# Joining the transfers of a convolution and Haar kernel: slanted filter rows, image blocks, channel parities, v with tau

## The chip, the cores and the metric

The kernel runs on one core of a Trainium2 chip. The metric is the device time of one execution in microseconds. Before the change the median of three runs is 2617.15 us (2612.36 to 2619.04). About 0.3% of that, some 8 us, is what a measurement of this kernel can tell from no change.

## What is computed

A tensor x of 4 images, 64 channels and 256 x 256 points (float32) goes through four layers. Layers 0, 2 and 3 are long convolutions whose filter is an outer product of a row filter and a column filter for each channel, so that each is a product with a Toeplitz matrix along the columns and then one along the rows, and `+ x * bias[c]`. The filters themselves come from a small network of three sines:

```python
h = sin(freq * (z @ w1 + b1)); h = sin(freq * (h @ w2 + b2)); h = sin(freq * (h @ w3 + b3))
hx = (h @ wo) * decay          # the same for hy with Y weights
k[c, i, j] = hx[i, c] * hy[j, c]
y = irfft2(rfft2(x) * rfft2(k)) [:256, :256] + x * bias[c]
```

Layer 1 works in the two-dimensional Haar domain, with two sets of weights i:

```python
f1 = haar2d(x)
for i in range(2):
    f4 = einsum("bchw,oc->bohw", f1 * v[i], conv_w[i])
    acc += sign(f4) * relu(abs(f4) - tau[i])
x = haar2d(acc, inverse=True) + x
```

## The kernel before, in words

The work is cut into rounds. A round holds two images (a group) and CI = 2 channels, as a tile of 128 partitions by 8 x 256; there are 64 rounds, 32 for each of the two groups. Three kinds of work follow each other and partly run side by side, in an order that Python loops write out (`beside` interleaves two lists of pieces, with no scheduler behind it):

- Phase A, for each round: layer 0 as two Toeplitz products on TensorE (`rows` into the PSUM tile a1ps, `columns` into a2ps, 128 matmuls each), the residual on VectorE (L449), the Haar butterflies along the free axis on GpSimd (L333, L335), the Haar product a3ps on TensorE, its scaling on VectorE (L462), and a store of the coefficients to DRAM (L466).
- Phase B, for each group and each of 64 steps: a step loads one slab of coefficients (L528, ft), v and tau (L539), mixes channels on TensorE (L579), multiplies by v (VectorE, L594), takes sign and magnitude (ScalarE, L598, L602), subtracts tau and thresholds (VectorE, L605, L608), adds up on GpSimd (L620 to L624), and stores to the DRAM tensor `mixed` (L629). Before its first mix, `join` finishes the Haar transform of steps 0 and 1 on VectorE (L551 to L558).
- Phase C, for each round: loads from `mixed` (L692, g), inverse Haar (GpSimd L370, ScalarE L353, TensorE c0ps), and layers 2 and 3 as Toeplitz products (c1r, c1c, c2r, c2c), with copies on ScalarE (L733) and residuals on VectorE (L752), and a store to `out` (L759).

In time: A runs alone up to some 450 us, A beside B of group 0 up to 1030 us, a transition to C up to 1200 us, C beside B of group 1 up to 1930 us, and C alone to the end.

The Toeplitz matrices are made by DMA. `spread` (L248) writes each channel's filter, zero padded to PERIOD = 320, REPEATS = 20 times into the DRAM tensor `filt`, and `load_toeplitz` (L139) reads it back with a slanted pattern (partition p starts p elements earlier), 64 partitions at a time, into tx (both X filters of a round) and ty (the Y filters). For rounds 0 and 1 `repeated` (L212) computes the copies directly, ahead of the network's last layer.

All DMAs are issued by the queue of SyncE (SP), in the order of the program; each takes one of eight semaphores in turn and so waits for the DMA eight places before it. What an issue also waits for is a buffer (tx and ty have 5, ft 4, v and tau 3, the x and g tiles 3) or data (a filter row that has landed in `filt`, coefficients). The lists `rest` and `thirds` (L270 to L274) place the `spread` calls of later quarters, and the networks of layers 2 and 3, between the pieces of phase A.

## Time and profile before

The profiled execution took 2622.7 us; its span, first to last instruction, is 2620.6 us, so 2.1 us lie around it.

| | busy us | share of the span |
|---|---|---|
| TensorE matmul (PE) | 2357.1 | 90% |
| TensorE weight load (PEld, overlaps PE) | 1908.0 | 73% |
| GpSimd (POOL) | 1951.1 | 74% |
| VectorE (DVE) | 1686.6 | 64% |
| ScalarE (ACT) | 1325.3 | 51% |

The granted TensorE clock is 0.965 on average. The DMA engines moved 631.58 MB in 241180 packets, 241 GB/s on average; the hardware queue's packets fill 69.4% of the 16 engines' span. Of a DMA the profile tells the issue (an instruction of SPq, the queue of SyncE), its count and its KB. A share of busy time is an average over stages whose limits differ, so it is read stage by stage.

### The profile page before, as it was taken

Reading aid. Unit: us, or ns where it says so; the run is one execution under the profiler, and the core shown is the slowest. Engines: PE = TensorE matmul, PEld = TensorE weight load, DVE = VectorE, ACT = ScalarE, POOL = GpSimd, SP = SyncE. Lnnn points to the kernel's source line nnn. Section 1 sums busy time; section 2 is a strip of 40 time slices with the busy share of each in tenths; the row PEclk is TensorE's granted clock in tenths of the full one; section 3 lists DMA queues with packets and bytes.
Section 4 is the critical chain, followed back from the end, with each engine's and each line's share of the span. In section 5 each row is a group of like instructions: output and inputs, shape, how many; then the busy total and the mean of one; then the engine's idle time right before and its main releaser. Section 6 shows DMA issues by size and latency. Waiting matters only on the chain.

```text
span 2620.6 us, 120068 instructions
## 1 busy us (share of the span) xinstructions
PE 2357.1 (90%) x53276; PEld 1908.0 (73%) x53276; DVE 1686.6 (64%) x1972; ACT 1325.3 (51%) x2169; POOL 1951.1 (74%) x2422
## 2 busy tenths in 40 slices
PE   6989999678878778768999999999999999999999
PEld 4777777445544445546877777787789999999999
DVE  2464445799999999736877878878763333333333
ACT  1111112566666656426777776778763443434432
POOL 2877887888989989858888878888876565565661
PEclk9999999899899888979999999999999999999999
DMA  5756887698999889556888878888865544445442
GB/s 147 252 193 221 254 261 275 232 332 326 336 332 335 319 316 331 186 190 216 286 310 288 295 273 288 274 285 286 284 231 181 171 143 153 159 141 166 148 137 86
DMA packets 241180, 631.58 MB, mean 241 GB/s; under 512 B 42758, under 2 KB 125351, under 8 KB 224536
## 3 DMA queue, kind: packets, MB, share of 16 engines
q1 hardware_dynamic: 240664, 623.92, 69.4%
q8 instruction: 419, 6.86, 1.1%
q14 instruction: 97, 0.79, 0.1%
HBM read 412.59 MB, written 211.16 MB: 238 GB/s over the span
## 4 chain that ended last, share of the span: by engine, by line
PE 42%; DVE 12%; DMA 10%; POOL 9%; ACT 6%; issue 5%; SPq 2%; DVEq 0%; ACTq 0%; POOLq 0%
PE c1c L285 9%; PE c2r L285 9%; PE c2c L285 8%; PE c1r L285 8%; PE c0ps L297 3%; DVE a L605 3%; PE f L579 3%; DVE x L594 3%; POOL f L335 2%; POOL fw L333 2%; DVE m L608 2%; DMA ft<-coef 2%; ACT a L602 2%; DMA mixed<-gt 2%; DVE x L449 2%
## 5 line engine op out<-in xcount | busy, mean ns | idle before, releaser
L370 POOL TENSOR_TENSOR i<-i,g 128x16 f32<-128x16 f32 x744 | 395.1, 550 | 378.9 <-ACT g L353 359.9
L579 PE MATMUL f<-ft,mix 64*64 64x512 f32 x2048 | 326.4, 642 | 106.7 <-DVE x L594 84.5
L285 PEld LDWEIGHTS a1ps<-tx,x 64*64 64x64 f32 x8192 | 303.4, 140 | 132.9 <-DVE f L462 47.8
L602 ACT ACTIVATE a<-x 128x1024 f32<-128x1024 f32 x256 | 264.5, 1033 | 205.6 <-DVE m L608 205.6
L285 PE MATMUL a1ps<-tx,x 64*64 64x192 f32 (+3 forms) x8192 | 341.5, 309 | 29.3 <-DVE f L462 15.3
L605 DVE TENSOR_TENSOR a<-a,tau 128x1024 f32<-128x1024 f32 x256 | 314.3, 1228 | 79.9 <-ACT a L602 77.5
L285 PEld LDWEIGHTS c2r<-tx,cy 64*64 64x64 f32 x8192 | 319.1, 135 | 62.2 <-ACT ch L733 28.8
L598 ACT ACTIVATE m<-x 128x1024 f32<-128x1024 f32 x256 | 271.9, 1062 | 173.3 <-DVE x L594 112.4
L594 DVE TENSOR_TENSOR x<-f,v 128x1024 f32<-128x1024 f32 x256 | 311.7, 1218 | 61.1 <-PE f L579 56.4
L285 PEld LDWEIGHTS c1c<-ty,ch 64*64 64x64 f32 x8192 | 311.3, 133 | 53.4 <-ACT ch L733 29.8
L285 PE MATMUL c2r<-tx,cy 64*64 64x64 f32 (+3 forms) x8192 | 330.9, 301 | 13.6 <-ACT ch L733 10.9
L285 PE MATMUL c1r<-tx,z 64*64 64x128 f32 (+3 forms) x8192 | 326.7, 299 | 13.1 <-DMA tx<-filt 6.7
L285 PEld LDWEIGHTS c1r<-tx,z 64*64 64x64 f32 x8192 | 303.0, 134 | 46.4 <-issue 26.4
L285 PEld LDWEIGHTS a2ps<-ty,ay 64*64 64x64 f32 x8192 | 281.4, 135 | 74.1 <-issue 27.2
L285 PE MATMUL a2ps<-ty,ay 64*64 64x256 f32 (+3 forms) x8192 | 319.1, 301 | 12.5 <-ACT ay L429 9.1
L285 PE MATMUL c1c<-ty,ch 64*64 64x192 f32 (+3 forms) x8192 | 321.1, 298 | 7.0 <-ACT ch L733 6.2
L608 DVE SCALAR_TENSOR_TENSOR m<-a,m 128x1024 f32<-128x1024 f32 x256 | 313.0, 1223 | 19.5
L429 ACT COPY ay<-a1ps 128x512 f32<-128x512 f32 x256 | 137.0, 587 | 370.7 <-PE a1ps L285 370.3
L285 PE MATMUL c2c<-ty,ch 64*64 64x192 f32 (+3 forms) x8192 | 316.4, 297 | 3.6 <-issue 3.6
L285 PEld LDWEIGHTS c2c<-ty,ch 64*64 64x64 f32 x8192 | 303.2, 133 | 22.4 <-issue 10.9
L449 DVE SCALAR_TENSOR_TENSOR x<-x,bias_sb,a2ps 128x512 f32<-128x512 f32 x256 | 179.4, 743 | 214.1 <-POOL f L335 132.1
L620 POOL TENSOR_TENSOR gt<-gt,m 128x1024 f32<-128x1024 f32 x128 | 303.2, 2369 | 11.7 <-DVE m L608 10.2
(69 smaller groups left out, 3193.9 us busy)
## 6 DMA issues: line engine op xcount, KB each, us to landing
coef<-f SPq DMA_DIRECT2D x256, 256.0 KB, 4.4
ft<-coef SPq DMA_DIRECT2D x256, 256.0 KB, 6.2
v<-in_v SPq DMA_DIRECT2D x128, 512.0 KB, 5.9
tau<-in_tau SPq DMA_DIRECT2D x128, 512.0 KB, 6.6
mixed<-gt SPq DMA_DIRECT2D x256, 256.0 KB, 5.9
g<-mixed SPq DMA_DIRECT2D x256, 256.0 KB, 5.5
x<-in_x SPq DMA_DIRECT2D x63, 1024.0 KB, 8.5
out<-o SPq DMA_DIRECT2D x63, 1024.0 KB, 5.1
```

The source lines that it names most:

```text
L285: nc.tensor.matmul(ps[r][half(c), j % 2, k * ROW :], data[half(r), c, k, bass.ts(j, ROW)], t(r, c)[:, : N - k * ROW], start=k == 0, stop=k ...
L297: nc.tensor.matmul(ps[r][half(c)].rearrange("p h k -> p (h k)"), matrix[half(r)], pairs(r, c).rearrange("p h k -> p (h k)"), start=True, s ...
L370: engine.tensor_tensor(to, s, d, op)
L429: later(lambda y=y, ps=ps: nc.scalar.copy(y, ps))
L449: nc.vector.scalar_tensor_tensor(to, old, bias_sb[:, c : c + 1], ps, ALU.mult, ALU.add)
L579: nc.tensor.matmul(un[u]["f4"][half(q), b, :], mixers[0][half(r), bass.ts(i, C)], st[s]["f"][half(r), b], start=True, stop=True, tile_posi ...
L594: nc.vector.tensor_tensor(un[u]["x"], un[u]["f4"], both(u, "v"), ALU.mult)
L598: nc.scalar.activation(un[u]["m"], un[u]["x"], AF.Sign)
L602: nc.scalar.activation(un[u]["a"], un[u]["x"], AF.Abs)
L605: nc.vector.tensor_tensor(un[u]["a"], un[u]["a"], both(u, "tau"), ALU.subtract)
L608: nc.vector.scalar_tensor_tensor(un[u]["m"], un[u]["a"], 0.0, un[u]["m"], ALU.max, ALU.mult)
L620: nc.gpsimd.tensor_tensor(st[s]["g"], st[s]["g"], m, ALU.add)
```

## The change

Every kind of transfer that was cut in two or more is made one, or fewer:

- `filt` is laid out by round: for each round and each half r of the 128 partitions, 20 repeats of three filters side by side (X of the first channel, X of the second, Y of channel r). One slanted row of 896 elements then holds all three, and a round's Toeplitz data is 2 DMAs of 64 x 896 in place of 6 of 64 x 256, in one tile `toep` with 4 buffers.
- `spread` therefore writes each X filter twice, for r = 0 and r = 1: six DMAs for a quarter of a layer, each with 8 rounds (6 in the first) by 20 repeats by 320. Before it was two DMAs for each of three thirds of the repeats, with 16 channels each. `rest` has 77 entries in place of 44.
- `repeated` computes 120 rows (2 x 20 x 3) in place of 80 and stores them by one DMA in place of two.
- `all_rows` (coefficient stores of A, g loads of C) gives 2 pairs in place of 4: both image halves h in one.
- `step_of` (ft loads, mixed stores of B) gives one transfer in place of two: both channel parities e.
- v and tau are stacked on the host into one tensor and come by one DMA of 1 MB in place of two of 512 KB.

The program has 1245 DMAs in place of 2651. The order of the instructions on the compute engines is the same, apart from where the pieces of the second network stand in phase A.

```diff
@@ -56,7 +56,10 @@
 NL = len(CONV)
 
 PERIOD = N + ROW
+ITEMS = 3
+SPAN = ITEMS * PERIOD
 REPEATS = 20
+COPIES = 2 * REPEATS * ITEMS
 
 FIRST = 2
 
...
@@ -103,7 +106,7 @@
 
     coef = [coefficients(f"coef{g}") for g in range(GROUPS)]
     mixed = [coefficients(f"mixed{g}") for g in range(GROUPS)]
-    filt = [dram.tile([P, REPEATS, PERIOD], F32, tag=f"filt{l}", name=f"filt{l}") for l in range(NL)]
+    filt = [dram.tile([ROUNDS, 2, REPEATS, ITEMS, PERIOD], F32, tag=f"filt{l}", name=f"filt{l}") for l in range(NL)]
 
     def pool(name, bufs, stack=ctx, **kw):
         return stack.enter_context(tc.tile_pool(name=name, bufs=bufs, reuse_waits="tile", **kw))
...
@@ -140,20 +143,12 @@
 
 
 
-        tx = ac.tile([P, CI, N], F32, tag="tx", name=f"tx{l}_{t}", bufs=5)
-        ty = ac.tile([P, N], F32, tag="ty", name=f"ty{l}_{t}", bufs=5)
-
-        def rows(dst, w, e):
-            start = (w * C + t % ROUNDS * CI + e) * REPEATS * PERIOD
-            src = bass.AP(filt[l].tensor, filt[l].offset + start, [[PERIOD - 4, 16], [PERIOD - 1, 4], [1, N]])
-            nc.sync.dma_start(dst, src)
-
-        for e in range(CI):
-            for r in range(2):
-                rows(tx[r * ROW : (r + 1) * ROW, e, :], 0, e)
-        for e in range(CI):
-            rows(ty[e * ROW : (e + 1) * ROW, :], 1, e)
-        return tx, ty
+        both = ac.tile([P, SPAN - ROW], F32, tag="toep", name=f"toep{l}_{t}", bufs=4)
+        for r in range(2):
+            start = filt[l].offset + (t % ROUNDS * 2 + r) * REPEATS * SPAN
+            src = bass.AP(filt[l].tensor, start, [[SPAN - 4, 16], [SPAN - 1, 4], [1, SPAN - ROW]])
+            nc.sync.dma_start(both[r * ROW : (r + 1) * ROW], src)
+        return both
 
 
     early = ctx.enter_context(ExitStack())
...
@@ -211,14 +206,11 @@
 
         def repeated(r):
 
-            ps = mps.tile([4 * REPEATS, N], F32, tag="ps", name=f"mlp_first{r}")
+            ps = mps.tile([COPIES, N], F32, tag="ps", name=f"mlp_first{r}")
             nc.tensor.matmul(ps, wo_first_sb[:, r], st["h"][:, 0], start=True, stop=True)
             t = repeats[r]
             nc.vector.tensor_tensor(t[:, :N], ps, decay_first_sb[:, r], ALU.mult)
-            for w in range(2):
-                to = filt[0][w * C + r * CI : w * C + (r + 1) * CI].rearrange("c r e -> (c r) e")
-                nc.sync.dma_start(to, t[w * CI * REPEATS : (w + 1) * CI * REPEATS])
-
+            nc.sync.dma_start(filt[0][r].rearrange("h c k e -> (h c k) e"), t)
 
         def last():
             ps = mps.tile([P, n, N], F32, tag="ps", name=f"mlp_out{ls[0]}")
...
@@ -240,19 +232,20 @@
 
     filters = {}
     first_toep = []
-    repeats = [mp.tile([4 * REPEATS, PERIOD], F32, tag=f"first{r}", name=f"first{r}") for r in range(FIRST)]
+    repeats = [mp.tile([COPIES, PERIOD], F32, tag=f"first{r}", name=f"first{r}") for r in range(FIRST)]
     for t in repeats:
         nc.gpsimd.memset(t, 0.0)
-    QUARTER = C // 4
-
-    def spread(l, q, part=slice(0, REPEATS)):
-
-        begin = q * QUARTER if (l, q) != (0, 0) else FIRST * CI
-        for w in range(2):
-            s = slice(w * C + begin, w * C + (q + 1) * QUARTER)
-            src = filters[l][s].unsqueeze(1)
-            times = part.stop - part.start
-            nc.sync.dma_start(filt[l][s, part], src.to_broadcast([src.shape[0], times, PERIOD]))
+    QUARTER = ROUNDS // 4
+
+    def spread(l, q):
+
+        begin, end = q * QUARTER if (l, q) != (0, 0) else FIRST, (q + 1) * QUARTER
+
+        def put(r, k, channel):
+            src = filters[l][channel + CI * begin : channel + CI * (end - 1) + 1 : CI].unsqueeze(1)
+            nc.sync.dma_start(filt[l][begin:end, r, :, k], src.to_broadcast([end - begin, REPEATS, PERIOD]))
+
+        return [lambda r=r, k=k: put(r, k, k if k < CI else C + r) for r in range(2) for k in range(ITEMS)]
 
     first_x = [load_x(0)]
     forward_sb = const.tile([P, ROW], F32, tag="forward", name="forward_sb")
...
@@ -267,11 +260,10 @@
     for p in network([0]):
         p()
 
-    thirds = [slice(0, 7), slice(7, 14), slice(14, REPEATS)]
-    rest = [lambda q=q, k=k: spread(0, q, k) for q in range(1, 4) for k in thirds]
+    rest = [p for q in range(1, 4) for p in spread(0, q)]
     rest.append(lambda: wbd_sb.extend(constant(f"wbd{l}", wbd[:, l], [P, 3, P]) for l in (1, 2)))
     rest += network([1, 2])
-    rest += [lambda l=l, q=q, k=k: spread(l, q, k) for l in (1, 2) for q in range(4) for k in thirds]
+    rest += [p for l in (1, 2) for q in range(4) for p in spread(l, q)]
 
     TILES = [(r, c) for r in range(2) for c in range(2)]
 
...
@@ -304,10 +296,10 @@
             )
 
     def filters_x(toep):
-        return lambda r, c: toep[0][half(r), c]
+        return lambda r, c: toep[half(r), c * PERIOD : c * PERIOD + N]
 
     def filters_y(toep):
-        return lambda r, c: toep[1][half(r)]
+        return lambda r, c: toep[half(r), CI * PERIOD :]
 
     def forward_free(src, dst, name):
 
...
@@ -393,13 +385,12 @@
     def all_rows(grp_tile, r, images):
 
 
-        parts = images.rearrange("(m q) (h n) k -> h q m (n k)", q=2, h=2)
+        parts = images.rearrange("(m q) (h n) k -> q m h (n k)", q=2, h=2)
         n = NB * W
         pairs = []
-        for h in range(2):
-            for q in range(2):
-                at = grp_tile.offset + ((h * 2 + q) * ROUNDS + r) * n
-                pairs.append((bass.AP(grp_tile.tensor, at, [[PAIR, P // 2], [1, n]]), parts[h][q]))
+        for q in range(2):
+            at = grp_tile.offset + (q * ROUNDS + r) * n
+            pairs.append((bass.AP(grp_tile.tensor, at, [[PAIR, P // 2], [2 * ROUNDS * n, 2], [1, n]]), parts[q]))
         return pairs
 
     def phase_a():
...
@@ -474,7 +465,8 @@
                     filters(1)
                     load(0)
                     load(1)
-                    spread(0, 0)
+                    for put in spread(0, 0):
+                        put()
                 filters(t + 2)
             if j < BLOCKS:
                 if t < total:
...
@@ -515,28 +507,25 @@
         def step_of(ap, s, images):
 
             n = NB * W
-            by_e = images.rearrange("(m e) b w -> e m (b w)", e=CI)
-            at = [ap.offset + (e * STEPS // 2 + s // 2) * PAIR + s % 2 * P // CI * n for e in range(CI)]
-            return [(bass.AP(ap.tensor, at[e], [[n, P // CI], [1, n]]), by_e[e]) for e in range(CI)]
+            at = ap.offset + s // 2 * PAIR + s % 2 * P // CI * n
+            rows = bass.AP(ap.tensor, at, [[n, P // CI], [STEPS // 2 * PAIR, CI], [1, n]])
+            return rows, images.rearrange("p b w -> p (b w)")
 
         def load_f(s):
             if s >= STEPS:
                 return
             d = st[s]
             d["f"] = bp.tile([P, NB, W], F32, tag="ft", name=f"ft_{grp}_{s}", bufs=4)
-            for rows, f in step_of(coef[grp], s, d["f"]):
-                nc.sync.dma_start(f, rows)
+            rows, f = step_of(coef[grp], s, d["f"])
+            nc.sync.dma_start(f, rows)
 
         def load_v(s):
             if s >= STEPS:
                 return
-            n = 2 * W
-            d = st[s]
-            for name, src in (("v", v), ("tau", tau)):
-                t = d[name] = bp.tile([P, 2, W], F32, tag=name, name=f"{name}_{grp}_{s}", bufs=3)
-
-                rows = bass.AP(src.tensor, src.offset + s * P * n, [[n, P], [1, n]])
-                nc.sync.dma_start(t.rearrange("p e w -> p (e w)"), rows)
+            n = 4 * W
+            t = bp.tile([P, 2, 2, W], F32, tag="v", name=f"v_{grp}_{s}", bufs=3)
+            st[s]["v"], st[s]["tau"] = t[:, 0], t[:, 1]
+            nc.sync.dma_start(t.rearrange("p k e w -> p (k e w)"), bass.AP(v.tensor, v.offset + s * P * n, [[n, P], [1, n]]))
 
         def four(name, at, b):
 
...
@@ -625,8 +614,8 @@
             un[u].clear()
 
         def store(s):
-            for to, g in step_of(mixed[grp], s, st[s]["g"]):
-                nc.sync.dma_start(to, g)
+            to, g = step_of(mixed[grp], s, st[s]["g"])
+            nc.sync.dma_start(to, g)
             st[s].clear()
 
         def piece(u, j):
...
@@ -907,9 +896,10 @@
     scaled = signs * w[order][:ROW, None] / math.sqrt(N)
     signs = signs * w[order][:ROW, None]
     pack = a["L1_conv_conv_w"].transpose(2, 0, 1).reshape(C, P)
-    v = by_row("v")
-
-    filters = [np.repeat([w * C + r * CI + e for w in range(2) for e in range(CI)], REPEATS) for r in range(FIRST)]
+    v = np.stack([by_row("v"), by_row("tau")], axis=2)
+
+    filters = [[r * CI, r * CI + 1, C + r * CI + h] for r in range(FIRST) for h in range(2)]
+    filters = np.tile(np.array(filters).reshape(FIRST, 2, 1, ITEMS), (1, 1, REPEATS, 1)).reshape(FIRST, COPIES)
     wo = _blocks(a[CONV[0] + "Xwo"], a[CONV[0] + "Ywo"])
     arrays = {
 
```

More of the change, by code (lines that the diff above doesn't have):

```diff
@@ L90, in conv_haar_kernel @@
 def conv_haar_kernel(
-    ctx: ExitStack, tc: tile.TileContext, x, zT, w1, wbd, cols, decay, wo_first, decay_first, bias, forward, inverse, wrow, pack, v, tau, out
+    ctx: ExitStack, tc: tile.TileContext, x, zT, w1, wbd, cols, decay, wo_first, decay_first, bias, forward, inverse, wrow, pack, v, out
 ):
@@ L172, in conv_haar_kernel @@
     wbd_sb = [constant("wbd0", wbd[:, 0], [P, 3, P])]
-    wo_first_sb = constant("wo_first", wo_first, [P, FIRST, 4 * REPEATS])
-    decay_first_sb = constant("decay_first", decay_first, [4 * REPEATS, FIRST, N])
+    wo_first_sb = constant("wo_first", wo_first, [P, FIRST, COPIES])
+    decay_first_sb = constant("decay_first", decay_first, [COPIES, FIRST, N])
     decay_sb = constant("decay", decay, [P, N])
@@ L946 @@
         "v": f(np.repeat(v[:, :, None], C, axis=2)),
-        "tau": f(np.repeat(by_row("tau")[:, :, None], C, axis=2)),
     }
```

## The prediction

> **What bounds the kernel now.** I read the busy times by stage first, because the change touches DMAs everywhere and a DMA is worth something only where an engine waits for one. Columns after the stretch: its length, then busy us of PE, PEld, DVE, ACT, POOL, then clock, DMA share, GB/s.

> ```profile
> 0.00:65.00 65.00, 38.91 (x745) 31.65 (x749) 17.71 (x37) 9.21 (x17) 13.03 (x24) 0.95 0.52 144
> 65.00:450.00 385.00, 357.72 (x8845) 285.25 (x8840) 197.30 (x293) 72.31 (x135) 312.02 (x521) 0.99 0.74 239
> 450.00:1030.00 580.00, 457.69 (x7473) 281.46 (x7471) 534.39 (x551) 359.36 (x448) 513.58 (x568) 0.91 0.88 318
> 1030.00:1200.00 170.00, 132.48 (x2338) 92.85 (x2334) 105.30 (x153) 62.66 (x96) 115.95 (x157) 0.87 0.59 209
> 1200.00:1930.00 730.00, 687.31 (x15236) 563.49 (x15228) 577.81 (x585) 549.31 (x883) 611.71 (x625) 0.99 0.81 283
> 1930.00:2621.00 691.00, 683.01 (x18676) 653.25 (x18668) 254.07 (x357) 272.42 (x594) 384.77 (x532) 1.00 0.47 150
> ```

> A alone is bound by PE (93%), A beside B by DVE (92%), C beside B by PE (94%), C alone by PE (99%). Only the start and the transition have an engine that nothing saturates. Next, the list of waits, for every engine wait that a DMA ended; these are its large entries (total, times, longest):

> ```profile
> DVE spare_f L551 <- DMA ft<-coef: 17.4, 1, 17.4
> ACT g L353 <- DMA g<-mixed: 16.0, 2, 12.6
> PE a1ps L285 <- DMA x<-in_x: 9.4, 2, 7.4
> PE c1r L285 <- DMA tx<-filt: 6.7, 1, 6.7
> ```

> With the smaller ones (3.4 for w_sb, 2.9 for tx, and some 25 us on DVE, ACT and POOL) that is all. So although the chain of waits gives DMAs 10% of the span, some 260 us, engines stood waiting for DMAs for about 80 us, and PE, which sets the end of most stages, for 22. The timeline shows two places. The start, with the SP queue:

> ```profile
> 28.37 0.59 SPq L136 DMA_DIRECT2D x<-in_x  x1
> 29.05 2.12 SPq L255 DMA_DIRECT2D filt<-padded  x2
> 36.21 3.51 SPq L149 DMA_DIRECT2D tx<-filt  x4
> 41.04 0.59 SPq L136 DMA_DIRECT2D x<-in_x  x1
> ```

> The x of round 2, issued at 41.04, is what PE waits 7.4 us for, until 50.0. It stood behind the filter rows of round 2, and these behind the landing of `spread` at 36.2. And the transition into C beside B:

> ```profile
> 1156.97 2.50 SPq L149 DMA_DIRECT2D tx<-filt  x4
> 1160.98 7.08 PE L285 MATMUL c1r<-tx,z 64*64 64x256 f32 x120 [6.73 <-DMA tx<-filt]
> 1166.16 4.96 SPq L528 DMA_DIRECT2D ft<-coef  x8
> 1170.55 0.42 DVE L551 TENSOR_TENSOR spare_f<-ft 64x256 f32<-64x256 f32 x1 [17.44 <-DMA ft<-coef]
> 1174.26 0.42 DVE L553 TENSOR_TENSOR spare_f<-ft 64x256 f32<-64x256 f32 x1 [2.83 <-DMA ft<-coef]
> ```

> Here SP issues back to back from 1151.95 on, one DMA in 0.6 us: the reader sees `ft` only reach the queue at 1166.16.

> [...] tx takes 592 ns (median of 768), and the issues of all 2651 DMAs add up to some 1730 us, 77% of the time from 1200 to 1900. [...]

> **The change, part by part.** *Bytes and packets.* In the trace's packet records a packet of 1024 bytes takes 46 ns (median), 4096 takes 159, 8192 takes 309: nearly a straight line, 7 ns and 0.037 ns a byte. v with tau as 8192 in place of twice 4096 saves 9 ns of 318. A slanted row of 3584 bytes comes by the line to 140, against 3 x 46 = 138. So the DMA engines gain nothing by size, and the 88% of A beside B stays. Hidden by DVE there.

> *SP.* 1406 issues fewer. At 0.6 us each that frees 840 us of SP; if a joined issue costs 1.0 us (the first `spread` took 1.06 with 240 rows) still 340. Almost all is nothing on the path: in A alone x is issued when DVE releases its buffer (SP waits 50.8 us on L449 there) and 12 us, a round, before use, with 4.3 to 7.0 us left after landing in the five rounds where the trace tells the landing; in B, v and ft follow DVE's subtraction. Without that cover a late load would cost its lateness each round.

> *Start.* Before: rows of rounds 0 and 1 are 12 issues from 20.71 to 28.3, then x of round 1 at 28.37. After: 4 issues, x at about 24. PE's wait for that x, 2.0 us at 33.6, goes. `spread` then starts 4.3 us earlier (24.7), but holds 720 packets of 1280 bytes in place of 480[...] it lands between 35 and 42, before 36.2. Two issues and one `spread` later x of round 2 is issued at 37 to 44 (before 41.04). With the same 9 us PE starts round 2 at 46 to 53 in place of 50.0. I take the middle with x landing faster, as less is queued beside it: -3 us (+3 to -6).

> *A alone.* `spread` has 66 DMAs of 160 packets, 2.46 in a round of 11.85 us[...]. x is issued first in the round and has 4 us or more to spare: 0, with a bad end below. The 4 buffers of `toep` add no wait in A: they wait for `columns` two rounds back, which precedes the DVE release that the x load ahead already waits for.

> *Transition.* The joined coefficient store must wait for both halves h, so for the last of the four L462 (end 1153.12); the two halves went from 1151.95 to 1154.36. Two issues of 0.6 from 1153.2 end at the same 1154.4. Then g takes 2 issues in place of 4 (1155.6) and the rows 2 in place of 6: the first lands by its 3.9 us at 1159.5 to 1160.5, as the same 2 MB are ahead of it in the engines. PE's 6.73 shrinks by 1. Then rows of layer 3 and the mixer, 3 issues; ft follows at about 1159 (coefficients must have landed) in place of 1166.16, 4 issues. Both steps land by 1167, so `join`, whose last wait ended at 1174.26, ends 7 us sooner. PE waited for it 4.5 us in two pieces (the list has `PE f` on `DVE ft`: 3.5 at 1179.28). These go, and nothing in PE's order before that mix needs it: 1 + 4.5. After it PE waits 4.8 us at 1229 for GpSimd's ci, which starts behind ScalarE's copies of the same mix: half a microsecond of that. Sum -6 (-1 to -11: nothing of join, or all three waits).

> *C beside B.* PE is idle 43 us of 730, mostly on ScalarE's c1r and c2r copies. The DMA waits there (4.6 DVE, 4.5 ACT before it, 8.9 POOL, 1.6 DVE) reach PE in part. I take a fifth of the 15 after 1200: -3 (0 to -8). The 4 buffers make layer 3's rows wait for the end of the last round's columns, not its middle; the next thing in the queue, the `out` store, waits longer than that, and the rows are due over a round later. Freeing v with tau costs nothing: the tau load already came second.

> *C alone.* PE 99%: 0.

> Sum: -3 - 6 - 3 = -12. Against the profiled 2622.7 that is 2610.7. That execution is 5.5 above the median of the runs, so the median becomes 2617.15 - 12 = 2605.

> **Rivals.** (1) *Hidden anyway*: `spread` lands late at the start (+2), and the transition only trades ft for g and ScalarE (-3): 2616. For it: 80 us of waits in 2620, most off PE. Against it: the two PE waits stand plainly at DMAs. (2) *SP's order matters everywhere*: with SP free, half of PE's 43 us in C beside B goes (-20) beside the 9: 2588. For it: SP is 77% busy there and in order, and the chain of waits runs through its issues. Against it: the engines' own lists name compute. (3) *Slower[...]*: [...] +38 - 12: 2643. [...] For it: the mean in A alone is already 112. [...]

> **How the numbers follow.** Main case 0.56, own range 2594 to 2612; hidden 0.23 (2609 to 2620); more 0.08; slower 0.13. The range 2588 to 2620 holds main and hidden and little else, 8 in 10. Faster by over 0.3% (below 2609.3): 0.52 + 0.08 = 0.60. Within: 0.04 + 0.23 = 0.27. Slower (above 2625): 0.13.

> **What would show it.** Round 2's first a1ps before 50.0; the first join of group 1 within 1168 and no PE wait for it; PE idle of C beside B 40 or less; A's round still 11.85 us with no a1ps wait for x; DVE still 92% from 450 to 1030; C alone 691. Wrong if a1ps waits for x or toep in A, or if the joined issues take 1.2 us or more.

## The result and the profile after

The changed kernel takes 2639.47 us (median of 4 runs, 2634.71 to 2646.05) against 2616.24 of the kernel before beside it: ratio 1.0092 [1.0063, 1.012]. Run again later it gave 1.0075 [1.0056, 1.0094]. The kernel before, timed once more beside itself (`before_again`), gave 1.0003 [0.9993, 1.0014], so a ratio of 1.002 or more whose interval lies clear of 1 is more than the same kernel shows against itself. The forecast was 2605, a gain of 12 us; the change loses 16 to 23.

What the change does to the queue came as computed. SP's issues fill 31% of the span in place of 66%, and a joined issue takes 0.33 to 0.85 us (median, by kind). The granted clock is 0.965 as before. The busy times by stage of the kernel after (columns as in the prediction; it runs some 10 to 24 us later than before from the third line on, so the stretches do not hold quite the same work):

```profile
65.00:450.00 385.00, 350.00 (x8474) 290.14 (x8466) 184.21 (x275) 69.01 (x129) 297.66 (x499) 0.98 0.71 243
450.00:1030.00 580.00, 456.68 (x7583) 279.04 (x7582) 532.84 (x554) 353.05 (x440) 513.02 (x574) 0.93 0.88 320
1200.00:1930.00 730.00, 684.72 (x15165) 560.47 (x15160) 575.13 (x582) 545.26 (x878) 608.00 (x622) 0.99 0.79 289
1930.00:2644.00 714.00, 698.58 (x18934) 654.12 (x18926) 265.70 (x370) 279.96 (x602) 396.37 (x541) 1.00 0.46 152
```

In A alone PE executed 8474 matmuls in the same 385 us, 371 fewer than before, and the DMA engines were less busy (0.71, before 0.74) though they moved slightly more. PE was held up, and not because the DMA engines were busier. The list of waits of the kernel after, its entries that answer to those shown of before, and one that did not seem worth showing there:

```profile
ACT g L345 <- DMA g<-mixed: 21.0, 2, 16.0
PE a2ps L277 <- issue: 20.3, 18, 2.4
DVE spare_f L540 <- DMA ft<-coef: 13.0, 1, 13.0
PE c1r L277 <- DMA toep<-filt: 7.9, 1, 7.9
PE a1ps L277 <- DMA x<-in_x: 7.3, 2, 6.3
```

The waits for DMAs are about what they were. New is the second line: in 18 places PE stood still in the middle of a column product, 20.3 us in all, with nothing that the profile shows to release it ("issue"). The kernel before has this entry too, but small:

```profile
PE a2ps L285 <- issue: 3.3, 5, 1.4
```

So the time did not go into a wait for data.

One profiled execution is worth about 10 us either way (the two of the unchanged kernel differ by 9.4 us in span; profiled times stand 10 us below to 10 us above the median of their kernel). I therefore compare stages, from two executions of each kernel, by the starts of PE's first product of a round (the end is that of PE's last product):

| stretch (us) | before, twice | after, twice | change of the mean |
|---|---|---|---|
| to A's round 2 | 50.0, 47.2 | 47.9, 47.6 | -0.9 |
| A's rounds 2 to 40 (A alone but for the last) | 518.9, 518.0 | 535.8, 529.7 | +14.3 |
| A's round 40 to C's round 0 (A beside B) | 568.9, 568.2 | 568.7, 569.5 | +0.6 |
| C's rounds 0 to 2 (transition) | 59.2, 60.1 | 53.0, 56.4 | -5.0 |
| C's rounds 2 to 28 (C beside B) | 702.9, 697.2 | 706.6, 705.5 | +6.0 |
| C's rounds 28 to 31 (end of B) | 70.1, 70.0 | 74.9, 76.1 | +5.5 |
| C's round 31 to the end (C alone) | 645.7, 645.6 | 652.4, 653.4 | +7.3 |

The sum is +27.8, of which the medians of the timed runs show 16 to 23. A alone, C alone and the end of B are far outside what the two executions of one kernel differ by; in C beside B the two of before differ by 5.7 themselves, so that the +6.0 there leans on the stalls and on the parts below.

### The profile page after: what moved, and what is told of

The parts are those of the page before. It is cut to its first block, busy times and chain, and to the rows that moved or that the text cites. A ratio compares the mean times of both kernels' runs of the same rounds, so it can differ in the third digit from the quotient of the medians.

```text
span 2644.3 us, 117882 instructions
## 1 busy us (share of the span) xinstructions
PE 2365.8 (89%) x53276; PEld 1913.8 (72%) x53276; DVE 1686.7 (64%) x1972; ACT 1325.5 (50%) x2169; POOL 1950.8 (74%) x2422
## 4 chain that ended last, share of the span: by engine, by line
PE 48%; DVE 16%; POOL 13%; ACT 7%; issue 6%; DMA 4%; SPq 1%; DVEq 0%; ACTq 0%; POOLq 0%
PE c2r L277 9%; PE c1c L277 9%; PE c2c L277 8%; PE c1r L277 7%; POOL fw L325 4%; DVE a L594 4%; POOL f L327 4%; PE a2ps L277 3%; DVE x L583 3%; PE c0ps L289 3%; PE a1ps L277 3%; DVE m L597 3%; PE f L568 3%; DVE x L440 2%; ACT a L591 2%
## 5 line engine op out<-in xcount | busy, mean ns | idle before, releaser
L277 PEld LDWEIGHTS a1ps<-toep,x 64*64 64x64 f32 x8192 | 309.1, 139 | 120.0 <-DVE f L453 41.7
L277 PEld LDWEIGHTS c2r<-toep,cy 64*64 64x64 f32 x8192 | 318.8, 135 | 76.9 <-ACT ch L722 35.5
L594 DVE TENSOR_TENSOR a<-a,v 128x1024 f32<-128x1024 f32 x256 | 314.5, 1229 | 81.4 <-ACT a L591 80.7
L277 PE MATMUL a1ps<-toep,x 64*64 64x64 f32 (+3 forms) x8192 | 341.5, 309 | 24.8 <-DVE f L453 10.1
L277 PE MATMUL a2ps<-toep,ay 64*64 64x256 f32 (+3 forms) x8192 | 329.1, 303 | 34.3 <-issue 20.3
L277 PE MATMUL c2r<-toep,cy 64*64 64x64 f32 (+3 forms) x8192 | 336.3, 302 | 24.5 <-ACT ch L722 14.8
L277 PEld LDWEIGHTS c1c<-toep,ch 64*64 64x64 f32 x8192 | 307.8, 133 | 61.4 <-ACT ch L722 28.4
L277 PE MATMUL c1c<-toep,ch 64*64 64x192 f32 (+3 forms) x8192 | 325.2, 298 | 9.7 <-ACT ch L722 4.8
L277 PE MATMUL c1r<-toep,z 64*64 64x64 f32 (+3 forms) x8192 | 321.6, 298 | 9.8 <-DMA toep<-filt 7.9
L277 PE MATMUL c2c<-toep,ch 64*64 64x128 f32 (+3 forms) x8192 | 318.6, 297 | 4.8 <-issue 4.6
L277 PEld LDWEIGHTS c2c<-toep,ch 64*64 64x64 f32 x8192 | 299.1, 133 | 29.4 <-issue 14.9
```

What stands on the lines that cost most here:

```text
L277: nc.tensor.matmul(ps[r][half(c), j % 2, k * ROW :], data[half(r), c, k, bass.ts(j, ROW)], t(r, c)[:, : N - k * ROW], start=k == 0, stop=k ...
L594: nc.vector.tensor_tensor(un[u]["a"], un[u]["a"], both(u, "tau"), ALU.subtract)
```

## The mechanism that the traces point to

The stalls have an address. I count PE's instructions from the start, loads included, in blocks of 256; the list of queues below gives that number. Of PE's waits that are shown as "issue" and last over 0.25 us, those at instruction 193 or 194 of a block number 18 and 21 in the two executions of the kernel before, and 45 and 49 in those of the kernel after. I call these stalls. All others, 7 or 8 in each of the four, stand before mixes of A beside B, at places of the program that answer to each other, and come to 10 to 12 us in each kernel alike. And the page's list of queues has this line, of the kernel after:

```profile
q8 instruction: 418, 6.85, 1.0%
```

Its packets have 16,384 bytes each, and their number fits PE's instructions in both kernels: 107,180 by 256 are 418.7 here, and 107,448 by 256 are 419.7 in the kernel before, which has 419 such packets. Each of the stalls ends 2.2 to 2.9 us after the start of such a packet. I read this as PE having run out of instructions and waiting for the next 16 KB. It is a reading of the counts and of the fixed place; no view names the engine that a packet is for.

How late the packet starts tells whether a stall follows. I took for each packet the place that PE had reached in the packet's block when it started, and whether PE then stalled at 193 of the next block, over A alone (65 to 450 us), C beside B and C alone (C's rounds 2 to 28, and 31 to the end). A place above 256 lies in the next block already:

| packet starts at instruction | before, twice: packets, followed by a stall | after, twice |
|---|---|---|
| below 330 | 556, 0 | 473, 0 |
| 330 to 369 | 57, 11 | 92, 29 |
| 370 or later | 35, 25 | 78, 60 |

No packet that started below 330 was followed by a stall, and three of four that started from 370 on were. The late ones double. What had gone ahead of them stands in the packet records. The largest delay in C alone of the kernel after: the packet started at 2092.25, when 296 data packets of 3584 to 8192 bytes had started since the place where a prompt one starts (instruction 165); SP had issued toep, toep, out, g and g in one go. In A alone the late ones lie behind x, toep, toep, the filter copies, coef and coef. In what order the DMA engines serve their queues the trace does not show.

It does let the backlog be counted: the bytes of all DMAs issued so far, less those of the data packets that have started. I took it at the moment when PE reaches instruction 165 of a packet's block. Where 1000 KB or more stood in the queues, 33 of 146 packets before and 84 of 275 after were followed by a stall; where there was less, 3 of 502 and 5 of 368. In A alone its median was 322 and 399 KB before, 1030 and 1051 after. So a backlog of this size goes with stalls in both kernels, and the change makes it nearly twice as frequent.

The join changed the density. 512 KB in one issue of some 0.6 us is a supply of 870 GB/s, and 16 engines with 4096 bytes in 159 ns (the median of both kernels) take 410, by an estimate from these times. Cut in 256 KB at 0.6 us, or in rows of 64 KB, SP supplied about what the engines took, or less; only x and out came 1 MB at a time, and v and tau 512 KB. **Theory 1**: SP's slow issuing spaced the data out, and joined transfers let the queues fill ahead of PE's instructions. The rivals: **R1**, the prediction's own third rival, that `spread` in its new shape is slow by itself; the bytes or the sizes cost by themselves, wherever they are; or SP's order and its waits for data carry it. Each expectation says in its own words which rival it means.

## The experiments

**One part alone.** `slanted_only` is the kernel before with the changed `filt`, `spread`, `repeated` and `load_toeplitz`; `blocks_only` with the changed `all_rows`; `parity_v_only` with the changed `step_of`, `load_f`, `store` and `load_v`; their diffs are the hunks of the change.

> The kernel before with only the filter part of the change: slanted rows of 896 in one tile, filt laid out by round, six spread DMAs for a quarter. Coefficient stores, g and ft loads, mixed stores, v and tau stay as before. Theory 1 (backlog: TensorE's instruction fetch, a 16 KB packet on its own queue, waits behind data that SP issues faster than the DMA engines drain it; the burst is x, then rows, then coefficients): part of the burst in A remains (x, then 2 row DMAs in place of 6 spread over 3.6 us), so A alone loses some 4 to 9 of the 14 us; C alone keeps its g loads of 256 KB and loses at most 2 us. Total 2618 to 2628. Rival R1 ([...]as in the prediction's third rival) and rival R2 (slanted rows of 3584 bytes are slow to fetch): all 14 us of A alone are here; under R2 C alone also loses its 6 to 11 us. Total 2630 (R1) or 2640 (R2).

> The kernel before with only the image blocks joined: coefficient stores of A and g loads of C as 512 KB in place of 256 KB; filters, ft, mixed, v and tau as before. Theory 1: in C alone the burst out, g, g (2 MB issued in 1.7 us, 5 us of engine time) stands as in the changed kernel: TensorE stalls with no releaser the profile shows in c2r, +5 to +8 us there; in A alone the coefficients come after six row issues, so +2 to +6. Total 2622 to 2630. R1 and R2: nothing in A and nothing in C, 2616 (within 0.3%).

> The kernel before with only phase B's joins: ft loads and mixed stores in one for both parities, v with tau. Theory 1: A alone and C alone as before (no change in their DMAs); at the transition ft reaches the queue 2.5 us sooner than before (4 issues in place of 8), so -2 to -4; no loss in B, where other engines than TensorE are the bound and its instructions are used up at half the rate. Total 2611 to 2616. If long transfers are bad in B too, 2620 or more. R1 and R2: the same as theory 1.

Measured: 1.0022 [1.0012, 1.0032], 1.0036 [1.002, 1.0052] and 1.0033 [1.002, 1.0045]. Each part loses, and they add to 0.91%. By stages, against the mean of before: slanted rows +13 in A's rounds 2 to 40, -7 in the transition, +5 in C alone; blocks +9 in C alone, nothing in A; parities and v +11 in C beside B, and +5 and +4 in A and in A beside B, of which nearly all of the 5 falls ahead of B, where their edit changes nothing, and shows how far one execution can stray. Three unrelated edits lose in three places, where each makes a stretch of traffic denser. Each missed in part what Theory 1 expected: `slanted_only` was to lose 4 to 9 us in A (its +13 is what R1 expected), `blocks_only` to lose in A too, and `parity_v_only` to gain.

**v with tau.** `v_tau_only` joins these and keeps the two parities apart:

```diff
-            for name, src in (("v", v), ("tau", tau)):
-                ...
-                nc.sync.dma_start(t.rearrange("p e w -> p (e w)"), rows)
+            t = bp.tile([P, 2, 2, W], F32, tag="v", name=f"v_{grp}_{s}", bufs=3)
+            ...
+            nc.sync.dma_start(t.rearrange("p k e w -> p (k e w)"), ...)
```

> The kernel before with v and tau in one transfer of 1 MB a step, all else as before. If the 9 us that the parities and v with tau together lost in C beside B come from v with tau, which issues 1 MB in one go: ratio 1.002 to 1.004 and stalls of PE in C beside B of 20 us or more (before 9.2, both joins together 31.0). If they come from ft and g of a step (twice 512 KB in place of four times 256): ratio 0.999 to 1.001, stalls 7 to 13 us.

Measured: 1.0027 [1.0013, 1.0041], C beside B +7, and 18.0 us of stalls there against 8.7 and 9.1. The stalls fall short of the 20 expected, the time agrees: v with tau, 1 MB in one issue, carries 7 of the 11 us, and about half of the stalls that `parity_v_only` adds (28.1 us in all).

**R1: spread in another shape.** `spread_wide` is the changed kernel with the copies of layers 2 and 3 written as 16 rounds by 10 repeats in place of 8 by 20.

```diff
-            nc.sync.dma_start(filt[l][begin:end, r, :, k], src.to_broadcast([end - begin, REPEATS, PERIOD]))
+            nc.sync.dma_start(filt[l][begin:end, r, part, k], src.to_broadcast([end - begin, times, PERIOD]))
```

> The changed kernel, with the spread DMAs of layers 1 and 2 as 16 rounds by 10 repeats in place of 8 rounds by 20 (same number, same bytes[...]). R1: the 13 us lost between rounds 15 and 33 of A alone mostly go, 2628. Theory 1: the burst x, rows, coefficients is the same; A alone gets back at most 4 us, 2635 to 2640. R2: 2639.

(Its layers 1 and 2 are the kernel's own numbers for layers 2 and 3.) Measured: 1.0068 [1.005, 1.0086], with 17.2 us of stalls in A alone, as with the change; A's rounds 2 to 40 take 527.3 us, 2.4 less than the better execution of the change. So R1's 13 us did not come back. R1 falls by its premise too: its packets of 1280 bytes, feared at 112 to 174 ns (the mean in A alone and the slowest tenth of before), took 60 ns on average in the change (275 to 440 us), against 114 and 104 before.

**More bytes, close and apart.** Both kernels are the kernel before with 1 MB more a round in C alone, at two places of the queue.

```diff
+            e = extra[0].tile([P, 2 * M, N], F32, tag="extra", name=f"extra_{t}", bufs=2)
+            nc.sync.dma_start(e, x[t // ROUNDS, t % ROUNDS])
```

> The kernel before, with an additional transfer in C alone: right behind each store of out, 1 MB of x is read once more into a buffer that nobody uses, ahead of the g loads (some 33 MB in 33 transfers, one issue of 0.6 us each; what is computed is unchanged). It makes the stretch of densely queued traffic, out and g, half as long again. Theory 1 (TensorE's next 16 KB of instructions queues behind dense data and comes too late): PE stalls at instruction 193 of 256 rise in C alone from 1.8 us to between 6 and 25 us, and C alone becomes 5 to 25 us longer, ratio 1.002 to 1.010. Rival (only the time that SP spends on issues, or waits of data, matter; one issue of 0.6 us a round in a stage where PE is 99% busy costs nothing): ratio 0.999 to 1.001.

> As extra_burst, with the same additional 1 MB a round in C alone, issued behind the layer 3 rows, some 5 us ahead of the store of out, when the queues are nearly empty (what is computed is unchanged). Theory 1 (dense stretches delay TensorE's instructions): fewer stalls than in extra_burst by at least half, C alone 0 to 5 us longer than before, ratio 0.999 to 1.003. Rival (the bytes themselves cost time, wherever they are): the same as extra_burst within 0.1%.

Measured: 1.0114 [1.0087, 1.014] and 1.0078 [1.0057, 1.01]. The first is just past the expected end, with C alone 25 us longer and 19.2 us of stalls in it; the second missed its expectation, with 21 and 16.0. PE's waits in C alone, first of `extra_burst`:

```profile
PE c2r L285 <- issue: 12.8, 11, 1.9
PE c1c L285 <- issue: 3.8, 7, 1.2
PE c1r L285 <- issue: 1.0, 1, 1.0
```

and of `extra_quiet`:

```profile
PE c1r L285 <- issue: 9.5, 9, 2.4
PE c2r L285 <- issue: 3.8, 5, 2.0
PE c2c L285 <- issue: 1.9, 1, 1.9
```

The kernel before has about 2 us there in all. Bytes that nobody waits for, with one issue a round, stop a PE that is 99% busy: that is Theory 1's claim in its plainest form. Instruction packets that meet a backlog of 1000 KB at instruction 165 number 11 and 10 in C alone of before and 49 in `extra_burst`, and its 19 stalls all follow such packets. Why the second missed is seen in SP's timeline of `extra_quiet`:

```profile
1998.49 0.58 SPq L685 DMA_DIRECT2D extra<-in_x  x1
1999.17 0.38 SPq L766 DMA_DIRECT2D out<-o  x1
1999.65 2.85 SPq L699 DMA_DIRECT2D g<-mixed  x4
...
2056.45 0.58 SPq L685 DMA_DIRECT2D extra<-in_x  x1
2060.98 0.34 SPq L766 DMA_DIRECT2D out<-o  x1
```

At first the load was not apart: SP was late and out followed at once. Rounds 31 to 34 hold 11.4 of its 16.0 us of stalls. From round 35 to the end, with 4 us or more between, it takes 575.5 us against 567.2 and 566.0 before, and `extra_burst` 586.4. So apart costs less than half of close, but not nothing: the rival that the bytes themselves cost keeps a part. Of its 15 stalls only 6 follow such a backlog, so the count at that one moment does not account for all.

**g apart from out.** `g_apart` is the changed kernel with g of the rounds of C alone issued by ScalarE later in the round; the same transfers, the same sizes. It changes two things at once, the moment and the queue: these packets show as a second data queue in its trace.

```diff
-            if j == 2 * BLOCKS and t + 3 != alone:
+            if j == (12 if t + 3 > alone else 2 * BLOCKS) and t + 3 != alone:
                 load(t + 3)
...
-                nc.sync.dma_start(g, rows)
+                (nc.scalar if t > alone else nc.sync).dma_start(g, rows)
```

> The changed kernel, with the g loads of group 1 issued by ScalarE in the middle of the round, in place of SP right behind the store of out; the same transfers with the same sizes, so that the 2 MB of out and g no longer follow each other. Theory 1: of the 6.0 us of stalls at instruction 193 in C alone at least 4 go and C alone gets 4 to 10 us shorter: ratio to before 1.009 less 0.002 to 0.004, 1.005 to 1.007. Rival (a joined transfer is slow by itself[...]): C alone unchanged or longer by ScalarE's issues, ratio 1.008 to 1.011.

> The changed kernel once more, beside g_apart_again on the same chip. Both theories: ratio to before 1.007 to 1.011.

> The kernel g_apart once more, beside the changed kernel. Theory 1 (dense stretches delay TensorE's instructions): 0.002 to 0.005 below after_again in the ratio, 5 to 12 us, and in the profile 2 to 4 us of stalls at instruction 193 in C alone against 5 to 8. Rival (the earlier difference came from the chip or the call): within 0.001 of after_again.

Measured: 1.0054 [1.0034, 1.0074] the first time; side by side 1.0065 [1.005, 1.0079] against 1.0075 [1.0056, 1.0094]. Beside each other the two totals are not told apart, and `g_apart_again` missed its 0.002 to 0.005. The stage tells them apart: C alone takes 647.7 and 647.0 us, against 652.4 and 653.4 of the change, and the stalls there fall from 6.0 and 6.3 us to 2.6 and 1.8. PE's waits in C alone, of `after_again`:

```profile
PE c2r L277 <- issue: 5.9, 9, 0.9
PE c2r L277 <- ACT ch L722: 4.1, 1, 4.1
```

and of `g_apart_again`:

```profile
PE c2r L277 <- issue: 2.0, 4, 0.9
PE c2c L277 <- issue: 0.2, 1, 0.2
```

Packets that start at 370 or later fall from 7 and 8 to 0 and 1. Packets that meet a backlog of 1000 KB at instruction 165 fall from 25 and 25 to 13 and 16. The transfers kept their size and lost most of their cost in the stage, so it is not the joined transfer by itself that costs. Whether the later moment, which breaks up the dense stretch, or the second queue did it, these runs do not separate.

**Spacing put back.** Three ways to thin the traffic in A: `paced` is the changed kernel with a small DMA (64 words) behind each joined one (two behind a joined row); `rows_split` is `slanted_only` with each slanted row read as three pieces; `x_out_split` is the kernel before with x and out in four pieces of 256 KB.

```diff
 # paced
+            nc.sync.dma_start(t, bass.AP(v.tensor, v.offset, [[1024, 16], [1000, 4], [1, 1]]))
 # rows_split
-            nc.sync.dma_start(both[r * ROW : (r + 1) * ROW], src)
+            for k in range(ITEMS):
+                ...
+                nc.sync.dma_start(both[r * ROW : (r + 1) * ROW, k * PERIOD : k * PERIOD + N], src)
 # x_out_split
-        n = BLOCKS if t == 0 else 2 * M
+        n = 2
```

> The changed kernel with every joined transfer kept, and behind each one as many tiny DMAs (64 partitions by one element, from the v tensor, into a scratch tile) as were joined into it: SP again makes as many issues as in the kernel before, at the old spacing, and its eight semaphores again cover half the bytes. Theory 1 as a backlog (SP issues joined transfers faster than the engines drain them, and TensorE's next 16 KB of instructions queue behind): the stalls at instruction 193 of 256 fall back to about those of before, and the gain at the transition goes too; 2612 to 2624. Theory 1 as length alone ([...]longer transfers hold the instructions up however they are spaced): no gain, 2636 or more. R1 and R2: no gain either, 2638.

> The filter part of the change alone (layout by round, six spread DMAs[...], half again as many bytes), but a round's rows read as 6 DMAs of 64 x 256 as before. Theory 1: reading in six is what paced the burst after x, so A alone is back within 3 us of before; 2615 to 2621. R1: the spread stays as changed, so the 8 to 9 us of the filter part stay; 2625. R2: gone, as the rows are short again; 2617.

> The kernel before with the longest transfers, x loads and out stores of 1 MB, cut into four of 256 KB. Theory 1 as a backlog: the bursts x, rows and out, g become flatter only a little (four issues of 0.33 us in place of one), so 0 to -4 us, mostly stalls in A alone and C alone; 2612 to 2617. Theory 1 as length alone: [...]all stalls of A and C alone go, with what GpSimd's and ScalarE's waits owe to them: -4 to -8; 2609 to 2613. R1 and R2: 2617.

Measured: 1.0323 [1.0303, 1.0344], 1.0147 [1.013, 1.0164] and 1.0055 [1.004, 1.0069]. All three expectations of a gain missed, though the stalls in A alone did fall: from 19.5 to 6.2 us, from 18.3 to 5.0, from 3.1 to 1.1, and in `x_out_split` no packet of A alone or C alone meets a backlog of 1000 KB. What took their place is seen in part in PE's waits in A alone, of `x_out_split`:

```profile
PE a1ps L285 <- DMA x<-in_x: 7.4, 8, 1.9
PE a1ps L285 <- DMA tx<-filt: 6.0, 5, 2.1
PE a2ps L285 <- issue: 1.1, 2, 0.7
```

and of `rows_split`:

```profile
PE a1ps L278 <- DMA toep<-filt: 6.3, 4, 2.9
PE a1ps L278 <- DMA x<-in_x: 2.9, 2, 2.5
```

So these runs show that thinner traffic takes stalls away, and not that it saves time. SP's issues fill 77 to 84% of A alone in these three, and 72% in the kernel before, 48% in the change. I read this as a second limit just above the kernel before: a few more issues, and x and the rows come late. The granted clock was lower too, in the mean of A alone 0.951 in `paced` and 0.960 in `rows_split`, against 0.987 before; what part of the loss goes with it, and whether it fell because PE waited, these runs do not show. `slant_late` runs into the limit from the other side. It slants only the filters of layers 2 and 3, and reads those of layer 0 by six loads as before (its expectation calls them layer 1), into the `toep` tile with its 4 buffers:

```diff
+        if l:
+            for r in range(2):
+                ...
+                nc.sync.dma_start(both[r * ROW : (r + 1) * ROW], src)
+            return both
```

> The kernel before, with only the filters of layers 2 and 3 in slanted rows (written in A by 48 of the changed kernel's spread transfers, read in C by 2 loads in place of 6); the filters of layer 1, read in A, are as before. Theory 1 (the joined reads, in dense stretches, cost): A as before within 3 us, transition 5 to 8 us shorter, C alone 3 to 7 us longer: ratio 0.998 to 1.001. Rival (A loses by the spread of the later layers, with its 1280-byte packets[...]): A 8 to 12 us longer as with all filters slanted, ratio 1.002 to 1.005.

Measured: 1.0108 [1.0087, 1.013]; A's rounds 2 to 40 take 552.6 us, +34, and nearly all of it lies between rounds 20 and 35, where the copies for layers 2 and 3 are written. In that stretch it has 1.6 times the packets of 1280 bytes, and SP's issues fill 85% (275 to 440 us; before 78%). The rival's direction held, its reason did not: the packets were no slower (87 ns on average, before 114 and 104). Stalls at 193 come to 2.7 us only. PE waits 7.6 us there for x and rows by the list, and 12.2 us in three waits without a shown releaser, each before a round's first product and 9.4 us after the issue of that round's x (x lands 8.5 us after its issue in the median of before). The granted clock in A alone was 0.951, worth some 14 us by an estimate from 0.987 and the 385 us. So I read the loss as late x and rows behind a busier SP, with the slower clock; no run here separates the two.

**The transition by order alone.** `ft_early` puts the opening loads of B's second half ahead of the rows of layer 3 and of g, all at their old sizes; `ft_ahead` leaves g in front; `ft_ahead_rows` puts the rows of round 1 in front of g.

```diff
                 filters(t + 1, 1)
+                if t == 0:
+                    b[0]()
                 filters(t, 2)
+                if t == 0:
+                    load(3)
...
-    beside(main, phase_b(1), ...
+    beside(main, [lambda: None] + b[1:], ...
```

> The kernel before with every transfer at its own size, and only the order on SP changed in the transition: the loads of mix, ft, v and tau that open the second half of B go ahead of the layer 3 rows of C's first round and of the g load of round 3. ft is then issued at about 1158 in place of 1166. If the gain of the transition is a matter of queue order: the tx wait of 6.7 falls to about 4 and the join ends 5 to 8 us sooner, ratio 0.996 to 0.999 (2608 to 2616 against 2618), faster than both kernels. If the gain needs fewer bytes or issues in flight: ratio 0.999 to 1.001. It is slower if the layer 3 rows, now some 7 us later, are what c2r of round 0 waits for, by 1 to 4 us.

> The kernel before, all transfers at their own size; in the transition only the six layer 3 rows of C's first round go behind the loads of mix, ft, v and tau, and g stays ahead. ft is issued at about 1161.5 in place of 1166.2. If the transition is a matter of queue order: the join's wait of 17.4 us on ft falls to 12 or 13, from C's first round to its third 54 to 57 us in place of 59.2, ratio 0.997 to 0.9995. If it is not, or if c2r of round 0 then waits for its rows: 59 us or more, ratio 0.9995 to 1.002.

> As ft_ahead, with the six layer 2 rows of round 1 also ahead of the g load of round 3. By queue order: PE's wait for those rows falls from 6.7 to 4 us, ScalarE's g comes 2 to 4 us later; from C's first round to its third 52 to 57 us, ratio 0.996 to 0.9995. Slower than ft_ahead if ScalarE's wait for g, behind which its copies for PE queue, exceeds 6 us: then 59 us or more and 1.000 to 1.003.

Measured: 1.004 [1.0025, 1.0055], 1.0028 [1.0016, 1.0039] and 1.0033 [1.0021, 1.0045]; none of the hoped-for gains came. The transition grew to 69.8, 65.0 and 65.0 us, from 59.2 and 60.1. Where it went, in ScalarE's waits of `ft_early`, 1150 to 1200 us:

```profile
ACT g L353 <- DMA g<-mixed: 27.7, 1, 27.7
```

and in PE's waits of `ft_ahead`, 1120 to 1205 us:

```profile
PE c2r L285 <- DMA tx<-filt: 11.1, 1, 11.1
PE c1r L285 <- DMA tx<-filt: 6.7, 1, 6.7
```

In the first g, which ScalarE's copies for PE queue behind, came late; in the second the rows of layer 3, as its expectation feared, and in the third too (12.8 us). Everything in that queue is due soon, and order alone gave one wait for another. The gain of the change stands in `slanted_only`: its transition takes 52.9 us, the wait on ft is 12.8 and PE's wait for the mix is gone, with two row loads in place of six ahead of ft. With the parities joined alone it takes 58.3, and the wait on ft is still 17.1. That fewer issues are the reason is likely, but not shown: `slant_late`, with the same two loads, takes 57.2. Open too: the transitions' growth of 10, 5 and 5 us is near what the timed runs lose (10, 8 and 9), but the profiled executions of these three, with spans of 2614.8 to 2617.3 us, are no longer as a whole than the two of before (2611.2 and 2620.6).

> The kernel before, unchanged, in the place of an experiment. If the place costs nothing: ratio 0.999 to 1.001. If part of what the small edits lost is the place and not the edit: ratio 1.001 to 1.003, and every ratio of these experiments is to be read against it.

None of the versions beats the kernel before.

## Why the prediction was wrong, step by step

- **A alone, "0"**: wrong, +14.3 us. The step asked only whether data come in time, and they do: PE waits for no x and no row between 65 and 450 us. It left out the packets of the queue q8, by my reading PE's own instructions, which take 1.0% of the 16 engines' span. The line `PE a2ps <- issue` of before (3.3 us in 5 places) was the visible edge of it. Stalls there: 3.1 and 1.8 us before, 19.5 and 15.1 after, 14.9 more in the mean, which is all of the loss.
- **SP, "almost all is nothing on the path"**: the size of the relief was right (issues of 1730 us became some 830), the sign of its effect was not. The relief was put at nothing because no data were waited for; but by Theory 1 the slow issue was what spaced the data, and with the joined issues the backlog at instruction 165 in A alone grew from 322 and 399 KB to 1030 and 1051. This is the step that failed; A alone, C alone and most of C beside B follow from it.
- **C alone, "PE 99%: 0"**: wrong, +7.3 us, of which 4.5 are stalls (1.7 on average before, 6.2 after). PE is 99% busy there, and nothing covers a late packet: `g_apart` gave 5.6 us back.
- **C beside B, "-3"**: wrong, +6.0 in rounds 2 to 28, with stalls of 14.4 and 20.1 us against 8.7 and 9.1; PE's idle time from 1200 to 1930 us grew to 45 us where 40 or less was to show the gain. By `v_tau_only` most of the time goes with v with tau. And +5.5 at the end of B, from a wait that the prediction did not look for: each joined g load needs what all its parts needed. In SP's waits, 1940 to 1985 us, of the kernel after:

```profile
SPq L681 <- DMA mixed<-gt: 4.6, 1, 4.6
```

  Before it was 0.5 us. g of the first rounds now lands after the last mixed store as a whole, ScalarE waits 16.0 us for it (12.6 before), and PE 3.1 us for ScalarE's copy (c2r on ch; in the repeated execution 4.1), where before its waits for such copies came to 0.4. That leaves some 2 us of the 5.5 without a wait named here.
- **Transition, "-6"**: the size was right, -5.0, the working only in part. The wait on ft fell from 17.4 to 13.0 us, and PE's wait of 4.5 us for the mix went, as said. But PE's wait for the rows did not shrink by 1; it grew from 6.7 to 7.9. The kernel after, in order of time:

```profile
1172.49 2.48 SPq L150 DMA_DIRECT2D toep<-filt  x4
1175.70 2.75 SPq L520 DMA_DIRECT2D ft<-coef  x4
1178.01 6.95 PE L277 MATMUL c1r<-toep,z 64*64 64x256 f32 x122 [7.86 <-DMA toep<-filt]
1182.01 0.42 DVE L540 TENSOR_TENSOR spare_f<-ft 64x256 f32<-64x256 f32 x1 [12.99 <-DMA ft<-coef]
```

- **Start, "-3"**: not measurable. x of round 2 was issued at 40.18 in place of 41.04, and PE waited 6.3 us for it in place of 7.4, but the 50.0 us of round 2 that the step started from was 2.8 us above the other execution of the same kernel. Rows of round 2 followed the landing of `spread` at 35.7, within the 35 to 42 that the step gave; that range was the author's estimate, and no trace here shows what it rests on.
- **A beside B, "0"**: right, +0.6; VectorE is busy there for 532.84 us of 580.
- **The rivals**: the slower one forecast 2643, near the result, but through slow copies, which the packet times refute (60 ns where it feared 112 to 174); how slow copies were to make 2643 was the author's estimate, and its nearness is luck. The signs that were to show the prediction wrong did not appear as meant: no wait for x or toep in A beyond the two of the start, and joined issues at medians of 0.33 to 0.85 us, though single ones took 1.2 us or more in both kernels (117 of 1245 after, 201 of 2651 before). They were all signs of the mechanisms thought of. Of those that were to show it right, A's round of 11.85 us failed (11.9 in the mean of rounds 2 to 32 before, 12.5 and 12.3 after), and so did C alone.

## What to carry to other kernels

A slow queue of issues can be doing a service: here SP's issues went from 66 to 31% of the span, and PE's stalls from 18 and 21 to 45 and 49. Before joining transfers, ask what else uses the DMA engines in the moment that they fill, the queue of instruction packets first, and look for idle time of the saturated engine that nothing releases and that recurs at a fixed count of instructions (here 193 or 194 of 256). Joining transfers of 64 to 512 KB did not pay here: each of three joins lost 0.2 to 0.4%. And a joined transfer waits for the last of everything that its parts waited for: SP's wait for the last mixed store ahead of g grew from 0.5 to 4.6 us.
